# Neighbour attention on one core: the weighted values summed by TensorE instead of VectorE

## The chip, the cores and the metric

The kernel runs on one NeuronCore of a Trainium2 chip. The metric is the device time of one execution in microseconds (us). Three runs of the kernel before took 2073.58, 2077.10 and 2083.18 us; the median is 2077.1 us.

## The reference

There are 3327 nodes with 256 features each and an adjacency matrix that is about 0.24% full, so a node has some eight neighbours besides itself. The reference applies four layers. Layers 0, 2 and 3 are transformer layers over the graph, layer 1 is an average over neighbours that is not touched by the change. A transformer layer is, cut to what matters:

```python
qkv = layer_norm(x, g1, be1) @ w_qkv                 # 8 heads of 32
scores = jnp.einsum('nhd,mhd->hnm', q, k) * SCALE
scores = jnp.where(adj != 0, scores, -jnp.inf)
attn = jax.nn.softmax(scores, axis=-1)
out = jnp.einsum('hnm,mhd->nhd', attn, v).reshape(n, DIM)
x = x + out @ w_proj + b_proj
x = x + jax.nn.gelu(layer_norm(x, g2, be2) @ w1 + b1) @ w2 + b2
```

Everything is float32. Since the matrix is sparse, the kernel does not form the dense scores: it makes a list of neighbours for each node and gathers their keys and values.

## The kernel before

**Stages.** First the adjacency matrix is read, lists of neighbours are made, and the nodes are sorted by their number of neighbours (0 to 306 us in the profile). Then come block 0, the averaging layer, block 1 and block 2. A block is one transformer layer (function `block`). It works on 26 tiles of 128 nodes. Since the nodes are sorted, tile `t` needs at most `ROOM[t]` neighbours: 24 for tile 0, 14 for tile 1, 12 for tiles 2 and 3, down to 4 for tiles 24 and 25, and 228 in sum. The tiles are taken from the smallest to the largest, in ten groups: (25,24), (23,22), (21,20,19), (18 to 15), (14 to 11), (10 to 7), (6,5,4), (3,2), (1), (0).

**Gathering and scoring** (`scores`). A tile loads its own row of keys, values and queries (`own`, three buffers; an indirect load by GpSimd in block 0, a plain load on SyncE's queue in blocks 1 and 2). Its neighbours' keys and values come in units of four neighbours (`unit`, 128 x 4 x 512 float32), each neighbour by one indirect load that GpSimd issues (L546). There are ten unit buffers for the whole block, so the loads run ahead by as many units as are free. ScalarE copies the query into a PSUM bank (L571; two such banks), and the scores lie in the same bank. For each unit VectorE multiplies the keys with the query (L576) and sums over the 32 elements of a head (L577). Then it adds the mask (L591), takes the maximum (L593) and subtracts it (L595); ScalarE takes the exponential (L596).

**Weighing** (`weighed`) is called one tile later, after the scores of the next tile. VectorE sums the exponentials (L605), takes the reciprocal (L606) and scales them (L607). It multiplies the values of `own` and of every unit with them, in place for the units (L610). Then it adds up: full units to the first one (L622), the last, shorter unit as well (L626), the four rows of the first unit in two halvings (L630), and the result to the tile's output `o` (L631). A unit's buffer is free after its last addition.

**The rest of the block** (`project`, `feed_forward`, `end`, `scatter`) goes by groups. TensorE transposes `o` (L658), ScalarE copies the result to SBUF as `oT` (L659), and TensorE multiplies with `w_proj` (L664). VectorE adds it to `x` (L671); after a normalization TensorE transposes (L256) and runs the two feed-forward products (L685, L695), with ScalarE's GELU between them (L688). In block 0 the averaging layer's inputs follow, in block 1 the next layer's keys (L538, L540), and GpSimd scatters the rows (L837, L779, L711). These steps are put off by some tiles through the list `later`, so that they run beside the gathers of later tiles.

**What sets the order.** The framework schedules the instructions on each engine by their order in the program and by its estimate of when they are ready; at run time every engine takes its own queue strictly in that order. An engine that waits holds up all that stands behind it. Float32 products on TensorE appear as two matmul records each in the profile, transposes as one.

The PSUM banks of a block are: four for `mm`, two for `tr` and two for `qs`, which is all eight.

Of the kernel before, what the change touches and what calls it, by code (L numbers as in the profile page):

```python
# [19 lines left out]
BF = mybir.dt.bfloat16  # L20
HF = mybir.dt.float16
F32 = mybir.dt.float32
# [9 lines left out]
P = 128  # L32
CW = 512
N = 3327
DIM = 256
HEADS = 8
HD = DIM // HEADS
# [14 lines left out]
KC = DIM // P  # L52
# [4 lines left out]
SLOTS = 24  # L57
LW = 32
LV = SLOTS + 1
UNIT = 4  # L60
# [25 lines left out]
class Sparse:  # L86
# [5 lines left out]
    def __init__(self, ctx, tc, bad):  # L92
        self.tc, self.nc = tc, tc.nc
        nc = self.nc
        self.bad = bad
        const = ctx.enter_context(tc.tile_pool(name="fixed", bufs=1))
# [23 lines left out]
        self.own = [dram.tile([P, 3 * DIM], F32, tag=f"own{t}", name=f"own{t}") for t in range(NT)]  # L120
        self.ones3 = const.tile([3, P], BF, name="ones3")
        nc.vector.memset(self.ones3, 1.0)
        self.biases = const.tile([3, 6, DIM], BF, name="biases")
        self.to = const.tile([P, NT], U32, name="to")
        self.ranks = dram.tile([NP], F32, name="ranks")
# [426 lines left out]
    def scores(self, pool, pp, layer, t, held):  # L552


        nc = self.nc
# [10 lines left out]
            nc.sync.dma_start(out=own[:, : 3 * DIM], in_=self.own[t])  # L566
        if layer < 2:
            nc.scalar.copy(self.x[t], own[:, 3 * DIM :])
        bank = pp.tile([P, CW], F32, tag="qs", name="qs", bufs=2)
        query = bank[:, :DIM]  # L570
        nc.scalar.copy(query, own[:, 2 * DIM : 3 * DIM])  # L571
        s = bank[:, ds(DIM, (SLOTS + 1) * HEADS)].rearrange("p (j h) -> p j h", h=HEADS)
        units = []

        def dot(at, k, n):
# [20 lines left out]
        nc.scalar.activation(s[:, : J + 1, :], s[:, : J + 1, :], AF.Exp)  # L596
        return own, s, units

    def weighed(self, pool, t, own, s, units):

        nc = self.nc
        J = ROOM[t]
        wide = [P, J + 1, HEADS]
        total = pool.tile([P, HEADS], F32, tag="total", name="total", bufs=3)
        nc.vector.tensor_reduce(total, s[:, : J + 1, :].rearrange("p j h -> p h j"), AX.X, ALU.add)  # L605
        nc.vector.reciprocal(total, total)  # L606
        nc.vector.tensor_mul(s[:, : J + 1, :], s[:, : J + 1, :], total.unsqueeze(1).to_broadcast(wide))  # L607

        def weigh(to, v, at, n):
            nc.vector.tensor_mul(  # L610
                to.rearrange("p j (h d) -> p j h d", d=HD), v.rearrange("p j (h d) -> p j h d", d=HD),
                s[:, ds(at, n), :].unsqueeze(3).to_broadcast([P, n, HEADS, HD]),
            )

        o = pool.tile([P, DIM], F32, tag="o", name="o", bufs=5)
        weigh(o.unsqueeze(1), own[:, DIM : 2 * DIM].unsqueeze(1), 0, 1)
        for u, j0, n in units:
            v = u[:, :n, DIM:]
            weigh(v, v, 1 + j0, n)
        full = [u for u, _, n in units if n == UNIT]  # L620
        for u in full[1:]:
            nc.vector.tensor_add(full[0][:, :, DIM:], full[0][:, :, DIM:], u[:, :, DIM:])  # L622
        u = full[0]
        for r, _, n in units:
            if n < UNIT:
                nc.vector.tensor_add(u[:, :n, DIM:], u[:, :n, DIM:], r[:, :n, DIM:])  # L626
        n = UNIT
        while n > 1:
            n //= 2
            nc.vector.tensor_add(u[:, :n, DIM:], u[:, :n, DIM:], u[:, ds(n, n), DIM:])  # L630
        nc.vector.tensor_add(o, o, u[:, 0, DIM:])  # L631
        return o

    def block(self, layer, weights, then, ahead=None, last=None):

# [3 lines left out]
        with tc.tile_pool(name="bs", bufs=1) as pool, tc.tile_pool(name="bp", bufs=1, space=PSUM) as pp:  # L639
            begin, finish, write = then(pool, pp) if then else (None, None, None)  # L640
            held = self.held

            def attended(t, own, s, units):
                o = self.weighed(pool, t, own, s, units)
                return t, o

            def halves(name, n):

                banks = [pp.tile([P, CW], F32, tag="mm", name=name, bufs=4) for _ in range(0, n, 2)]
                return [banks[q // 2][:, ds(q % 2 * DIM, DIM)] for q in range(n)]  # L650

            def project(group, outs):
                w = len(group) * P
                ps = [pp.tile([P, CW], F32, tag="tr", name="otr", bufs=2) for _ in range(KC)]
                oT = pool.tile([P, KC, CW], F32, tag="hT", name="oT", bufs=2)
                for k in range(KC):
                    for q, (t, o) in enumerate(outs):
                        nc.tensor.transpose(ps[k][:, ts(q, P)], o[:, ts(k, P)], self.ident)  # L658
                    nc.scalar.copy(oT[:, k, :w], ps[k][:, :w])  # L659
                ys = halves("proj", len(group))  # L660
                for q, y in enumerate(ys):
                    self.bias(y, 2 * layer)
                    for k in range(KC):
                        nc.tensor.matmul(y, oT[:, k, ts(q, P)], wpj[:, k, :], start=False, stop=k == KC - 1)  # L664
                return ys
# [67 lines left out]
                        scatter(group, ys)  # L733
                    later.sort(key=lambda x: (x[0], -x[1]))

            waiting, step, outs = None, 0, []
            for group in [*GROUPS, ()]:
                for t in group or (None,):
                    now = t is not None and (group, t, *self.scores(pool, pp, layer, t, held))
                    if waiting:  # L740
                        done, *rest = waiting
                        outs.append(attended(*rest))
                        if len(outs) == len(done):
                            later.append((step + 1 + (len(done) > 2), 0, done, project(done, outs)))
                            later.sort(key=lambda x: (x[0], -x[1]))
                            outs = []
                    waiting = now
                    if begin and step == 2:
                        begin()
                    run(step)  # L750
                    step += 1
# [829 lines left out]
```

## Time and profile before

| What | Value |
| --- | --- |
| Median of three runs | 2077.1 us |
| Profiled execution, first to last instruction | 2094.6 us |
| Mean granted TensorE clock | 0.770 of full speed |
| VectorE busy | 1342.0 us (64%) |
| TensorE busy, matmuls | 1263.4 us (60%) |
| GpSimd busy | 1001.0 us (48%) |
| ScalarE busy | 684.9 us (33%) |
| Indirect loads of neighbours (L546), 684 | 667.2 us, 975 ns each |
| Dot products (L576, units and own), 276 | 244.0 us |
| Weighing (L610, units and own), 276 | 242.2 us |

The profile is one execution, taken by the hardware's profiler. PE is TensorE's matmuls, PEld its weight loads, DVE VectorE, ACT ScalarE, POOL GpSimd and SP SyncE. A line such as L546 is a line of the kernel before. In a row of a group, `out<-in` names the tiles, then come the shapes and the count; after the bar stand the busy time and the mean time of one in ns, after the next bar the idle time of that engine just before these instructions, with the work that ended it. The three blocks' 228 loads each lie at 314 to 760, 1071 to 1484 and 1609 to 2002 us; the rest of a block, until its last feed-forward is through, lasts until about 850, 1606 and 2095 us.

### The profile page before, as it was taken

To read this page: it belongs to the slowest core of one execution; us is meant where nothing else is said; L and a number is where in the kernel's file an instruction comes from. 1 tells how busy PE (TensorE), PEld (TensorE's weight loads), DVE (VectorE), ACT (ScalarE), POOL (GpSimd) and SP (SyncE) were. 2 spreads that over 40 slices of the span, in tenths; PEclk is the share of its full clock that TensorE was granted. 3 is DMA by queue.
4 is the path that set the end of the run, shared out by engine and by line. 5 is a ranking of instruction groups with operands and counts; after the bars stand their busy time and mean duration, and the time that the engine had idled before them with its cause. 6 is when DMAs were issued, how large, how long until landed. Compare 5 with 4: busy or idle time off the path is not lost. (4 is left out here: it accounts for less than half of the span.)

```text
span 2094.6 us, 17222 instructions
## 1 busy us (share of the span) xinstructions
PE 1263.4 (60%) x4806; PEld 812.1 (39%) x4806; DVE 1342.0 (64%) x3407; ACT 684.9 (33%) x1420; POOL 1001.0 (48%) x946
## 2 busy tenths in 40 slices
PE   3244411556755579699934688567695277655676
PEld 1122200344424337577512454343473154323445
DVE  3567635577776785165636789776732679976871
ACT  3555501233321224122322444334343133322232
POOL 3768757555555531101156645555203666565521
PEclk8667655677767769799976888798798587767778
DMA  8878827555555550858486656656215665565520
GB/s 191 330 300 326 284 79 213 160 163 154 170 148 175 147 131 23 198 154 230 160 284 205 216 166 209 220 178 193 61 56 201 210 186 176 176 190 160 152 65 20
DMA packets 169409, 369.73 MB, mean 177 GB/s; under 512 B 78821, under 2 KB 90291, under 8 KB 165976
## 3 DMA queue, kind: packets, MB, share of 16 engines
q0 software_dynamic: 68624, 222.01, 35.4%
q1 hardware_dynamic: 85689, 112.44, 17.1%
q10 hardware_dynamic: 14990, 34.08, 5.0%
q8 instruction: 40, 0.66, 0.1%
q14 instruction: 66, 0.54, 0.1%
HBM read 279.77 MB, written 77.59 MB: 171 GB/s over the span
## 5 line engine op out<-in xcount | busy, mean ns | idle before, releaser
L546 POOL DMA_INDIRECT unit<-kv,ids x684 | 667.2, 975 | 434.7 <-issue 189.1
L685 PE MATMUL f<-hT,w 128*128 128x256 f32 (+3 forms) x960 | 342.1, 517 | 58.6 <-ACT gT L688 23.2
L256 PE MATMUL tr<-ident,xh 128*128 128x128 f32 x312 | 80.6, 384 | 442.7 <-ACT xh L251 395.6
L695 PE MATMUL f<-w,gT 128*128 128x256 f32 x1248 | 306.4, 399 | 17.9 <-ACT gT L688 14.3
L685 PEld LDWEIGHTS f<-hT,w 128*128 128x128 f32 x960 | 190.4, 219 | 202.6 <-issue 106.0
L695 PEld LDWEIGHTS f<-w,gT 128*128 128x128 f32 x1248 | 238.3, 197 | 68.7 <-ACT gT L688 18.3
L256 PEld LDWEIGHTS tr<-ident,xh 128*128 128x128 f32 x312 | 41.7, 179 | 483.3 <-ACT xh L251 414.8
L576 DVE TENSOR_TENSOR unit<-unit,qs 128x1024 f32<-128x1024 f32 (+3 forms) x198 | 211.7, 1069 | 26.4 <-DMA unit<-kv,ids 15.0
L577 DVE TENSOR_REDUCE qs<-unit 128x32 f32<-128x1024 f32 (+3 forms) x198 | 212.7, 1074 | 4.8 <-DVE qs L607 1.7
L610 DVE TENSOR_TENSOR unit<-unit,qs 128x1024 f32<-128x1024 f32 (+3 forms) x198 | 210.0, 1065 | 0.0
L315 POOL TENSOR_TENSOR m<-a,place 128x3328 f16<-128x3328 fp8e4 x26 | 159.4, 6132 | 78.7 <-ACT a L313 78.6
L688 ACT ACTIVATE gT<-f,b 128x256 f32<-128x256 f32 (+3 forms) x240 | 124.8, 536 | 212.5 <-PE f L685 106.6
L538 PE MATMUL kvps<-wqkv,hT 128*128 128x512 f32 x312 | 171.9, 677 | 29.5 <-ACT hT L262 22.5
L326 DVE MAX8 found<-m 128x8 f16<-128x416 f16 x208 | 111.5, 579 | 39.7 <-POOL m L315 33.1
L664 PE MATMUL proj<-wproj,oT 128*128 128x256 f32 x312 | 109.3, 489 | 42.7 <-ACT oT L659 22.8
L576 DVE TENSOR_TENSOR own<-own,qs 128x256 f32<-128x256 f32 x78 | 32.3, 415 | 141.5 <-ACT qs L571 124.2
L658 PE MATMUL otr<-ident,o 128*128 128x128 f32 x156 | 25.5, 289 | 142.4 <-DVE qs L577 87.4
L990 POOL DMA_INDIRECT sorted<-st,to x26 | 24.8, 955 | 178.7 <-ACT st L542 147.1
L538 PEld LDWEIGHTS kvps<-wqkv,hT 128*128 128x128 f32 x312 | 63.2, 213 | 86.7 <-issue 37.7
L313 ACT ACTIVATE a<-a 128x3328 fp8e4<-128x3328 int32 x26 | 77.3, 2973 | 51.6 <-DMA kv<-st 29.0
L251 ACT ACTIVATE xh<-x,shift,rstd 128x256 f32<-128x256 f32 x104 | 58.4, 594 | 104.5 <-DVE shift L218 80.9
L664 PEld LDWEIGHTS proj<-wproj,oT 128*128 128x128 f32 x312 | 66.9, 235 | 65.6 <-ACT oT L659 28.4
(193 smaller groups left out, 1881.4 us busy)
## 6 DMA issues: line engine op xcount, KB each, us to landing
a<-in_adj SPq DMA_DIRECT2D x25, 1663.5 KB
kv<-st ACTq DMA_DIRECT2D x52, 512.0 KB
own<-sorted SPq DMA_DIRECT2D x26, 512.0 KB
unit<-kv,ids POOLq DMA_INDIRECT x684
adj<-a SPq DMA_DIRECT2D x26, 416.0 KB
own<-qkv SPq DMA_DIRECT2D x26, 384.0 KB
own<-own SPq DMA_DIRECT2D x26, 384.0 KB
w<-in_L_gnn_w SPq DMA_DIRECT2D x6, 1024.0 KB
```

The source lines that it names most:

```text
L256: nc.tensor.transpose(ps[k][:, ts(q, P)], t[:, ts(k, P)], self.ident)
L315: nc.gpsimd.tensor_mul(m.rearrange("p (s e) -> p s e", e=SEG), a8.rearrange("p (s e) -> p s e", e=SEG), place.unsqueeze(1).to_broadcast([P ...
L326: nc.vector.max(found[:, i, s, :], m[:, ts(s, SEG)])
L538: nc.tensor.matmul(kv, hT[:, k, ts(q, P)], w[:, k, DIM : 3 * DIM], start=k == 0, stop=k == KC - 1)
L546: g = self.nc.gpsimd.indirect_dma_start(out=out, out_offset=None, in_=table, in_offset=bass.IndirectOffsetOnAxis(ap=self.ids[:, t, j : j + ...
L576: nc.vector.tensor_mul(k, k, query.unsqueeze(1).to_broadcast([P, n, DIM]))
L577: nc.vector.tensor_reduce(s[:, ds(at, n), :].rearrange("p j h -> p (j h)"), k.rearrange("p j (h d) -> p j h d", d=HD), AX.X, ALU.add,)
L610: nc.vector.tensor_mul(to.rearrange("p j (h d) -> p j h d", d=HD), v.rearrange("p j (h d) -> p j h d", d=HD), s[:, ds(at, n), :].unsqueeze ...
L664: nc.tensor.matmul(y, oT[:, k, ts(q, P)], wpj[:, k, :], start=False, stop=k == KC - 1)
L685: nc.tensor.matmul(y[:, :w], w1[:, k, ts(f, P)], hT[:, k, :w], start=k == 0, stop=k == KC - 1)
L688: nc.scalar.activation(gT[-1][:, f % 2, :w], y[:, :w], AF.Gelu_apprx_tanh, bias=b1[:, f : f + 1])
L695: nc.tensor.matmul(y, gT[f // 2][:, f % 2, ts(q, P)], w2[:, f, :], start=False, stop=f == FC - 1)
```

## The change

The query is no longer copied: the dot products read it from `own` in SBUF. The scores lie in an SBUF tile with three buffers. The two PSUM banks of `qs` go to a tile `acc`. VectorE still multiplies the values with the weights, now in place for `own` too, but it no longer adds them up. Instead TensorE multiplies every weighted row of 128 nodes x 128 features with the identity and accumulates in `acc`, two products per neighbour (one for each half of the features), after one small product of ones and zeros that clears the tile. As the weighted rows are the stationary operand, `acc` comes out transposed, so the transposes (L658) go, and ScalarE copies `acc` of each tile into its part of `oT`. The lines below are numbered anew in the changed kernel.

```diff
+        self.zeros3 = const.tile([3, DIM], BF, name="zeros3")
+        nc.vector.memset(self.zeros3, 0.0)
...
-        bank = pp.tile([P, CW], F32, tag="qs", name="qs", bufs=2)
-        query = bank[:, :DIM]
-        nc.scalar.copy(query, own[:, 2 * DIM : 3 * DIM])
-        s = bank[:, ds(DIM, (SLOTS + 1) * HEADS)].rearrange("p (j h) -> p j h", h=HEADS)
+        query = own[:, 2 * DIM : 3 * DIM]
+        s = pool.tile([P, SLOTS + 1, HEADS], F32, tag="s", name="s", bufs=3)
...
+        acc = pp.tile([P, KC, P], F32, tag="acc", name="acc", bufs=2)
+        nc.tensor.matmul(acc.rearrange("p k r -> p (k r)"), self.ones3, self.zeros3, start=True, stop=False)
+
+        def weigh(v, at, n):
             nc.vector.tensor_mul(
-                to.rearrange("p j (h d) -> p j h d", d=HD), v.rearrange("p j (h d) -> p j h d", d=HD),
+                v.rearrange("p j (h d) -> p j h d", d=HD), v.rearrange("p j (h d) -> p j h d", d=HD),
                 s[:, ds(at, n), :].unsqueeze(3).to_broadcast([P, n, HEADS, HD]),
             )
-
-        o = pool.tile([P, DIM], F32, tag="o", name="o", bufs=5)
-        weigh(o.unsqueeze(1), own[:, DIM : 2 * DIM].unsqueeze(1), 0, 1)
+            for j in range(n):
+                for k in range(KC):
+                    nc.tensor.matmul(
+                        acc[:, k, :], v[:, j, ts(k, P)], self.ident, start=False, stop=at + j == J and k == KC - 1
+                    )
+
+        weigh(own[:, DIM : 2 * DIM].unsqueeze(1), 0, 1)
         for u, j0, n in units:
-            v = u[:, :n, DIM:]
-            weigh(v, v, 1 + j0, n)
-        full = [u for u, _, n in units if n == UNIT]
-        for u in full[1:]:
-            nc.vector.tensor_add(full[0][:, :, DIM:], full[0][:, :, DIM:], u[:, :, DIM:])
-        u = full[0]
-        for r, _, n in units:
-            if n < UNIT:
-                nc.vector.tensor_add(u[:, :n, DIM:], u[:, :n, DIM:], r[:, :n, DIM:])
-        n = UNIT
-        while n > 1:
-            n //= 2
-            nc.vector.tensor_add(u[:, :n, DIM:], u[:, :n, DIM:], u[:, ds(n, n), DIM:])
-        nc.vector.tensor_add(o, o, u[:, 0, DIM:])
-        return o
+            weigh(u[:, :n, DIM:], 1 + j0, n)
+        return acc
...
+            def attended(group, q, t, own, s, units):
+                acc = self.weighed(pool, pp, t, own, s, units)
+                if q == 0:
+                    turned[group] = pool.tile([P, KC, CW], F32, tag="hT", name="oT", bufs=2)
+                nc.scalar.copy(turned[group][:, :, ts(q, P)], acc)
...
-                ps = [pp.tile([P, CW], F32, tag="tr", name="otr", bufs=2) for _ in range(KC)]
-                oT = pool.tile([P, KC, CW], F32, tag="hT", name="oT", bufs=2)
-                for k in range(KC):
-                    for q, (t, o) in enumerate(outs):
-                        nc.tensor.transpose(ps[k][:, ts(q, P)], o[:, ts(k, P)], self.ident)
-                    nc.scalar.copy(oT[:, k, :w], ps[k][:, :w])
+                oT = turned.pop(group)
```

## The prediction

> **What bounds the kernel now.** I read the page's busy times first, then busy time by stretch, then the groups of the three blocks, then the waits.
>
> ```profile
> span 2094.6 us, 17222 instructions
> ...
> PE 1263.4 (60%) x4806; PEld 812.1 (39%) x4806; DVE 1342.0 (64%) x3407; ACT 684.9 (33%) x1420; POOL 1001.0 (48%) x946
> ```
>
> No engine fills the span, so the limit has to be found by stage. Each block has a gather phase (its 228 indirect loads) and a tail after the last of them; from the trace they lie at 314-760 and 760-850, 1071-1484 and 1484-1606, 1609-2002 and 2002-2095. Busy time in those stretches (columns: length, then busy time and count by engine, granted clock, DMA):
>
> ```profile
> core 0: us, PE busy (x) PEld busy (x) DVE busy (x) ACT busy (x) POOL busy (x), PEclk, DMA share, GB/s
> 314.00:584.00 270.00, 137.37 (x490) 92.24 (x491) 188.56 (x440) 77.41 (x179) 159.83 (x165) 0.71 0.59 173
> 584.00:760.00 176.00, 98.49 (x321) 61.24 (x321) 124.68 (x248) 43.19 (x106) 99.26 (x102) 0.70 0.54 155
> 760.00:850.00 90.00, 75.38 (x341) 54.42 (x341) 48.70 (x136) 35.23 (x98) 10.73 (x12) 0.86 0.29 77
> 1071.00:1340.00 269.00, 162.26 (x524) 100.69 (x525) 202.37 (x487) 98.97 (x227) 154.55 (x157) 0.75 0.65 205
> 1340.00:1484.00 144.00, 104.35 (x339) 61.54 (x337) 102.48 (x195) 51.06 (x100) 84.59 (x86) 0.88 0.61 192
> 1484.00:1606.00 122.00, 101.07 (x395) 67.46 (x395) 51.67 (x153) 57.53 (x145) 10.96 (x12) 0.89 0.25 82
> 1609.00:1825.00 216.00, 112.81 (x367) 72.87 (x368) 167.78 (x382) 62.03 (x131) 133.35 (x135) 0.69 0.63 194
> 1825.00:2002.00 177.00, 105.70 (x349) 65.34 (x347) 129.69 (x253) 40.60 (x83) 106.66 (x108) 0.75 0.57 167
> 2002.00:2095.00 93.00, 64.30 (x282) 45.90 (x280) 46.67 (x110) 29.60 (x71) 11.04 (x11) 0.85 0.09 26
> ```
>
> In the gather phases VectorE is busy 313 of 446, 305 of 413 and 297 of 393 us (70 to 76%). GpSimd is busy 259, 239 and 240; with the 0.3 us that it loses before every issue it is at 332, 307 and 307 (74 to 78%). TensorE has 236, 267 and 218 (53 to 65%). In the tails TensorE leads (69 to 84%). So a loop of VectorE, GpSimd and the ten unit buffers paces the gather phases, and the last feed-forwards on TensorE pace the tails.
>
> **The additions that go.** L622, L626, L630 and L631:
>
> ```profile
> L622 DVE TENSOR_TENSOR unit<-unit 128x1024 f32<-128x1024 f32 x66 | 80.2, 1216 | 0.0
> ...
> L630 DVE TENSOR_TENSOR unit<-unit 128x512 f32<-128x512 f32 (+1 forms) x156 | 86.1, 552 | 4.4 <-DVE qs L591 1.2 <-issue 1.1 <-DVE qs L577 1.0
> ```
>
> With L626 (37.0 us) and L631 (32.5) that is 235.8 us, 79 a block, of which 66 lie in the gather phase. VectorE's gather phases fall to 247, 239 and 231 us.
>
> **The query copies that go.** L571 costs ScalarE 29.2 us, and VectorE waits for it:
>
> ```profile
> DVE own L576 <- ACT qs L571: 124.2, 22, 24.4
> ...
> ACT qs L571 <- DVE unit L610: 78.2, 17, 14.1
> ```
>
> The copy waits for one of two PSUM banks, which the weighing (L610) of two tiles earlier gives back. The new dot reads `own` and an SBUF tile with three buffers, so this wait goes. What is late next is `own` itself in block 0 (ScalarE waits 86.5 us for it at L568 already), and elsewhere the gathers. The part that comes back is at most 124 us and at least nothing; it is inside the phase estimate below, not added to it. The per-tile copies of `acc` (78, by L571's 0.375 us some 29 us) replace 60 copies of 23.8 us, beside other work on ScalarE. But each is a new wait in ScalarE's queue: behind it stand the GELUs and the next exponential, and VectorE's L605 waits for that.
>
> **The products that come.** Per block 228+26 rows of values, two halves each: 508 products of 128x128 f32 and 26 zeroing products. Each f32 matmul of this kernel is two records (L695: 26 tiles x 8 x 3 blocks = 624 in the code, x1248 in the trace), while a transpose is one (L658: 52 x 3 = 156). The nearest row, the same shape at the full clock:
>
> ```profile
> 2064.14 3.84 PE L685 MATMUL f<-hT,w 128*128 128x128 f32 x32 [0.50 <-ACT hT L262]
> ```
>
> 3.84/32 = 0.12 us a record, 0.24 a product, 122 us a block; with 26 zeroings by the bias product's 0.12 us spacing (+3) and 52 transposes gone (25.5/3 = -8.5), +117 us. At half clock wider records of this line take twice as long (128x384: 2.93 us for four at 763.7, 4.14 for twelve at 781.7), so the other end is +230. I take +117, since a busier TensorE should hold its clock (0.85 to 0.89 in the tails, 0.70 to 0.75 where it is half idle). The Trainium skill ("TensorE: Matmul & The Clock Gate", Terms) calls transpose mode four times faster for fp32; an estimate by it, four records' time a product, makes 244 us a block. The trace's two records decide against it.
>
> Of the 122 us, tiles 1 and 0 (80 products, 19 us) fall into the tail, since in the new order they stand behind the feed-forward of (6,5,4) and of (3,2). The gather phases get 95: TensorE goes to 331 of 446, 362 of 413, 313 of 393 us, if nothing stretched. In block 1, which also makes keys, that is 88%. And TensorE moves into the buffer loop: a unit is free not after VectorE's addition but after its products, which stand in order behind a feed-forward. One for four tiles holds TensorE from 1959.6 to 1986.2, 27 us. `own` too is now given back by a product: the loads of the next `own`, on SyncE's queue in blocks 1 and 2 and on GpSimd's in block 0, wait for TensorE with it. The other way round, a product that waits for VectorE's weighing holds up the feed-forward queued behind it, and VectorE's L671 and GpSimd's scatters wait for that. These waits have no row of their own; the phase shares below carry them.
>
> **Both operands in SBUF.** Gathers take 0.946 us, unless VectorE is at an addition with both inputs in SBUF:
>
> ```profile
> 743.83 1.88 POOL L546 DMA_INDIRECT unit<-kv,ids  x1 [3.36 <-DVE qs L595]
> ```
> ```profile
> 743.67 1.22 DVE L622 TENSOR_TENSOR unit<-unit 128x1024 f32<-128x1024 f32 x1
> ```
>
> The gather that began 0.16 us into the addition took 1.88 us: it ends about 0.82 us after the addition. Over the trace a gather that starts inside such an instruction is lengthened by what remains of it less 0.125 us; none is lengthened by L576, L577 or L610, which have one operand in PSUM. After the change L576 and L610 (487 us) have both inputs in SBUF and the additions (236 us) are gone. Putting that rule on the old positions of all 788 indirect DMAs gives 26 us for the additions (the rows show 684 x 0.029 = 20 for the unit gathers) and 92 us for L576, L610 and the small score steps: +66 us, 22 a block, to GpSimd: 354, 329, 329 with its issue gaps. Bounds: -20 if the gathers fall into step with VectorE and nothing is left, and 684 x 0.41 (162 us of such instructions in a 400 us phase) x 0.49 us (mean remainder of 1.21 us less 0.125) = 137, so 117 more than now, if they start anywhere. I take the count on the real positions. The Trainium skill ("SBUF — State Buffer", Who interferes with whom) says the later of the two blocks for the whole instruction, and speaks against this change; by it the same count without the 0.125 us would be somewhat higher. VectorE itself loses nothing visible: 1.22 us at most under a gather.
>
> **The sum.** In the gather phases the busiest engine after the change is GpSimd (354), TensorE (362), GpSimd (329, TensorE 313). Now the best is 78% (GpSimd in block 2). At 78% the phases would be 454, 464 and 422 us: +8, +51, +29 = +88. At 88% they would be 402, 411 and 374: -44, -2, -19 = -65. Three engines near 80% in strict order will not reach the second; a rising clock shortens TensorE's older work and helps. I take 82.5%: 429, 439, 399, in sum +15. The tails are TensorE's: +19 us each, less the 7.5 us of additions after tile 0's weighing where TensorE waited for them; bounds 0 and 19, taken 12: +35. ScalarE's and SyncE's own queues: nothing added on the path. The two stages outside the blocks are untouched.
>
> Sum +50 us on the profiled execution's 2094.6 us span (the page shows no time around it): 2145. That execution is 17.5 us above the median of the runs, 2077.1, so the forecast is 2077.1 + 50 = 2127 us. A measurement of this kernel tells some 0.5% (10 us) from no change.
>
> **Rivals.**
> - *VectorE's relief comes through.* For it: VectorE is the busiest engine in the gather phases, loses a fifth there, and its 124 us wait for queries goes. Against: it leaves GpSimd at 329 to 354 and puts TensorE beside it. It decides from 86%: there the phases are 412, 421, 383 (-37), which the tails' +35 just cancel. At 90%, 393, 402, 366 (-91) and +35: 2021 us.
> - *The unit buffers wait behind TensorE.* Tiles of 9 to 12 gathers take three of the ten buffers, so little more than three tiles are in flight. At 22 us a tile (584-760 for the last eight or so) a 27 us feed-forward ahead of the products holds the buffers of one to two tiles; if GpSimd then stops for 12 us at four such places a block, that is 144 us, of which I count a third as inside the idle time that 82.5% leaves anyway: +96 over the sum's +50, 2223 us. It decides from about three stops a block. For it: GpSimd's waits for L622 and L631, which release units, are 119 us already. Against: tiles of up to 8 gathers take two buffers and have slack.
> - *Even.* Gain in blocks 0 and 2, loss in block 1 and the tails: 2077.
> - That the change does not do what it says is excluded by the program's own order: no addition is left on VectorE, and the products stand in TensorE's queue.
>
> **How the numbers follow.** Forecast 0.52 (2090 to 2185), relief 0.27 (1960 to 2066), unit buffers 0.13 (2185 to 2320), even 0.08. The range leaves out the lower part of the relief and the upper part of the buffers' case, about a tenth each: 2000 to 2205. Faster is the relief, 0.27; same is the even case, 0.08; slower the other two, 0.65.
>
> **What would show it.** No additions on VectorE, 288, 278 and 265 us of it left in the three blocks (367, 357, 344 now); 3048 new records on TensorE, near 0.12 us apart; gathers longer than 1 us in far more than 76 cases; TensorE above 75% in the gather phases with a clock above 0.8; GpSimd waiting for TensorE at the gathers instead of VectorE; tails longer by 10 to 20 us. Wrong if products run at half clock throughout (then slower), if the gathers keep 0.946 us, or if the gather phases fall below 400 us each (then VectorE was the limit).

## The result, and the profile after

The changed kernel took 2229.3 us (median of four runs, 2211.0 to 2236.4), the kernel before 2076.5 us on the same chip: 1.073 times as long, with a 95% interval of 1.066 to 1.079. The forecast of 2127 us had the sign right and was 102 us short; its range ended at 2205.

The profiled execution of the changed kernel, from its page:

```profile
span 2234.7 us, 22841 instructions
...
PE 1588.0 (71%) x7776; PEld 1170.7 (52%) x7776; DVE 1162.3 (52%) x3054; ACT 681.0 (30%) x1372; POOL 1081.4 (48%) x946
```

VectorE lost 180 us, TensorE won 325, and the span grew by 140. Busy time by stretch, each block from its first to its last gather and then its tail (columns as in the prediction):

```profile
core 0: us, PE busy (x) PEld busy (x) DVE busy (x) ACT busy (x) POOL busy (x), PEclk, DMA share, GB/s
313.00:792.00 479.00, 339.37 (x1658) 258.07 (x1659) 270.47 (x598) 126.82 (x274) 290.49 (x266) 0.82 0.52 155
792.00:880.00 88.00, 80.33 (x482) 67.73 (x480) 31.73 (x106) 31.41 (x90) 10.84 (x13) 0.97 0.31 78
1107.00:1588.00 481.00, 367.21 (x1720) 268.00 (x1721) 268.45 (x605) 152.50 (x334) 260.28 (x243) 0.85 0.55 173
1588.00:1699.00 111.00, 102.82 (x527) 78.16 (x525) 29.25 (x112) 48.49 (x118) 10.67 (x12) 1.00 0.27 92
1699.00:2134.00 435.00, 313.18 (x1556) 241.58 (x1556) 259.46 (x559) 105.19 (x206) 267.85 (x243) 0.83 0.55 164
2134.00:2235.00 101.00, 77.25 (x427) 63.14 (x427) 23.00 (x68) 27.53 (x62) 10.99 (x12) 0.87 0.09 24
```

The gather phases took 446, 413 and 392 us and take 479, 481 and 435: 143 us more, which is the whole loss. No engine is busy for more than 77% of any of them. GpSimd, which issues the gathers, is busy for 819 us in the three phases and was for 738: 80 of the 143 us are longer work on it, and 63 are longer waiting. Its 684 gathers, before and after, with their busy time, mean time and the idle time ahead of them:

```profile
L546 POOL DMA_INDIRECT unit<-kv,ids x684 | 667.2, 975 | 434.7 <-issue 189.1
```
```profile
L548 POOL DMA_INDIRECT unit<-kv,ids x684 | 739.8, 1082 | 468.0 <-issue 192.5
```

The waits of GpSimd, VectorE and ScalarE in the changed kernel (what waits, for what: us in total, times, longest):

```profile
POOL unit L548 <- PE acc L619: 186.4, 25, 27.7
...
POOL out L703 <- DVE x L663: 124.7, 10, 38.2
...
DVE unit L576 <- DMA unit<-kv,ids: 189.4, 64, 21.3
DVE x L663 <- PE f L687: 153.7, 30, 12.1
...
ACT oT L641 <- PE acc L619: 276.9, 36, 19.4
```

GpSimd waits 186 us for products (L619) before it may load into a unit again; before, it waited 119 us for the additions that freed units:

```profile
POOL unit L546 <- DVE o L631: 64.4, 11, 8.2
POOL unit L546 <- DVE unit L622: 54.7, 10, 14.3
```

With what is put down to other work, its waits of over 0.4 us at a unit's gather sum to 229 us in the three phases before and to 256 after. The rest of its new waiting is mostly in block 2, where scatters of finished rows (L703) stand in GpSimd's queue ahead of gathers and need the feed-forward's result. In that block's gather phase they cost more than the products, and 7.0 us before the change:

```profile
POOL out L703 <- DVE x L663: 49.9, 6, 16.0
POOL unit L548 <- PE acc L619: 35.2, 9, 27.7
```

VectorE waits 189 us for gathered units (15 before) and 154 us for feed-forward results (73 before). One wait for products, on TensorE's timeline (start, duration, then the work; `x` is the number of records):

```profile
523.52 1.51 PE L619 MATMUL acc<-ident,unit 128*128 128x128 f32 x8
524.88 7.03 PE L677 MATMUL f<-hT,w 128*128 128x512 f32 x16
534.56 8.83 PE L677 MATMUL f<-hT,w 128*128 128x512 f32 x16 [2.65 <-ACT gT L680]
...
543.53 3.72 PE L687 MATMUL f<-w,gT 128*128 128x256 f32 x16
...
555.12 3.72 PE L687 MATMUL f<-w,gT 128*128 128x256 f32 x16
558.67 2.17 PE L619 MATMUL acc<-ident,unit 128*128 128x128 f32 x18
```

The products stop at 525 us for a feed-forward of four tiles and go on at 558.67. By then VectorE had weighed six more units:

```profile
525.71 2.69 DVE L613 TENSOR_TENSOR unit<-unit,s 128x1024 f32<-128x1024 f32 x3
...
540.36 2.69 DVE L613 TENSOR_TENSOR unit<-unit,s 128x1024 f32<-128x1024 f32 x3
```

On GpSimd and on ScalarE in the same stretch:

```profile
559.33 0.95 POOL L548 DMA_INDIRECT unit<-kv,ids  x1 [24.78 <-PE acc L619]
```
```profile
560.88 0.37 ACT L641 COPY oT<-acc 128x256 f32<-128x256 f32 x1 [16.76 <-PE acc L619]
```

GpSimd had no free unit for 24.8 us and issued its next gather 0.7 us after the products went on. Over all 198 units, the lag, which is the time from a unit's weighing to the end of its last product, is 28.8, 31.9 and 28.2 us in the mean of the three blocks, and 57 at most. That matmuls keep their program order is also what the Trainium skill states ("PSUM — Partial Sum Buffer", Engine vs sequencer instructions); the row of 558.67 is what it costs here.

### The profile page after: what moved, and what is told of

Its sections match the earlier page's. It is cut to its first block, busy times and chain, and to the rows that moved or that the text cites. A ratio compares the mean times of both kernels' runs of the same rounds, so it can differ in the third digit from the quotient of the medians.

```text
span 2234.7 us, 22841 instructions
## 1 busy us (share of the span) xinstructions
PE 1588.0 (71%) x7776; PEld 1170.7 (52%) x7776; DVE 1162.3 (52%) x3054; ACT 681.0 (30%) x1372; POOL 1081.4 (48%) x946
## 4 chain that ended last, share of the span: by engine, by line
PE 45%; issue 12%; DMA 11%; DVE 11%; another core or an unknown queue 9%; ACT 6%; POOL 5%; SPq 0%; ACTq 0%; DVEq 0%; POOLq 0%
PE f L687 10%; PE f L677 10%; PE acc L619 9%; PE kvps L540 5%; POOL unit L548 4%; DMA kv<-st 4%; PE qps L542 2%; DVE unit L576 2%; DMA unit<-kv,ids 2%; DVE s L577 2%; PE proj L656 2%; PE tr L258 2%; DMA st<-in_x 2%; PE tf L966 1%
## 5 line engine op out<-in xcount | busy, mean ns | idle before, releaser
L548 POOL DMA_INDIRECT unit<-kv,ids x684 | 739.8, 1082 | 468.0 <-issue 192.5
L619 PE MATMUL acc<-ident,unit 128*128 128x128 f32 x2736 | 370.9, 292 | 45.3 <-issue 42.3
L619 PEld LDWEIGHTS acc<-ident,unit 128*128 128x128 f32 x2736 | 355.9, 208 | 54.6 <-issue 51.7
L576 DVE TENSOR_TENSOR unit<-unit,own 128x1024 f32<-128x1024 f32 (+3 forms) x198 | 212.6, 1077 | 236.2 <-DMA unit<-kv,ids 189.4
L677 PE MATMUL f<-hT,w 128*128 128x256 f32 (+3 forms) x960 | 301.9, 473 | 23.8 <-issue 11.2
L577 DVE TENSOR_REDUCE s<-unit 128x32 f32<-128x1024 f32 (+3 forms) x198 | 209.5, 1065 | 0.3
L613 DVE TENSOR_TENSOR unit<-unit,s 128x1024 f32<-128x1024 f32 (+3 forms) x198 | 205.0, 1073 | 0.0
L619 PE MATMUL acc<-ident,own 128*128 128x128 f32 x312 | 65.6, 338 | 131.2 <-DVE own L613 98.7
L619 PEld LDWEIGHTS acc<-ident,own 128*128 128x128 f32 x312 | 51.7, 229 | 169.1 <-issue 89.3
L576 DVE TENSOR_TENSOR own<-own 128x256 f32<-128x256 f32 x78 | 33.1, 424 | 158.5 <-DMA own<-kv,ids 48.2
```

What stands on the lines that cost most here:

```text
L548: g = self.nc.gpsimd.indirect_dma_start(out=out, out_offset=None, in_=table, in_offset=bass.IndirectOffsetOnAxis(ap=self.ids[:, t, j : j + ...
L576: nc.vector.tensor_mul(k, k, query.unsqueeze(1).to_broadcast([P, n, DIM]))
L577: nc.vector.tensor_reduce(s[:, ds(at, n), :].rearrange("p j h -> p (j h)"), k.rearrange("p j (h d) -> p j h d", d=HD), AX.X, ALU.add,)
L613: nc.vector.tensor_mul(v.rearrange("p j (h d) -> p j h d", d=HD), v.rearrange("p j (h d) -> p j h d", d=HD), s[:, ds(at, n), :].unsqueeze( ...
L619: nc.tensor.matmul(acc[:, k, :], v[:, j, ts(k, P)], self.ident, start=False, stop=at + j == J and k == KC - 1)
L677: nc.tensor.matmul(y[:, :w], w1[:, k, ts(f, P)], hT[:, k, :w], start=k == 0, stop=k == KC - 1)
```

## The experiments

Theory A says that this holding of units behind TensorE is the loss. Theory B puts it on the longer gathers (both operands of VectorE's products in SBUF), Theory C on the sum of TensorE's work, Theory D on ScalarE's copies of the sums, which wait in its queue ahead of later tiles' exponentials.

Kernels of one set ran on one chip, beside the kernel before. Chips differ: the kernel before took 1910 to 1914 us on the chips of four sets, 2088 on that of the third set, and 2076 where the result was measured. So ratios to the kernel before on the same chip are compared, and ratios of different sets only where these chips were alike. "Excess" is the time of the 684 unit gathers over 946 ns each.

### First set: one part alone, and less of the sums

The move to SBUF alone (`b_sbuf`):

```diff
-        bank = pp.tile([P, CW], F32, tag="qs", name="qs", bufs=2)
-        query = bank[:, :DIM]
-        nc.scalar.copy(query, own[:, 2 * DIM : 3 * DIM])
-        s = bank[:, ds(DIM, (SLOTS + 1) * HEADS)]...
+        query = own[:, 2 * DIM : 3 * DIM]
+        s = pool.tile([P, SLOTS + 1, HEADS], F32, tag="s", name="s", bufs=3)
```

> The kernel before with one part of the change alone: the queries are read where they land in SBUF and the scores are a tile in SBUF; ScalarE's 78 query copies go, VectorE's additions stay, TensorE gets no products. Theory A (units wait behind TensorE: the products stand in TensorE's order behind the feed-forward, so the ten unit buffers come free some 30 us later): this part brings only the longer gathers, some 60 to 75 us of GpSimd time over the three blocks, of which a part is hidden: 2077 to 2150 us, best guess 2110, and well below the 2229 us of the changed kernel. Theory B (VectorE's products with both operands in SBUF hold up GpSimd, and this alone is the loss): 2200 to 2230 us. Theory C (TensorE has too much work in the gather phases) as A.

Measured 1.038 (1.033 to 1.042), 72 us. The group of the gathers in that kernel, from its page:

```profile
L546 POOL DMA_INDIRECT unit<-kv,ids x684 | 820.1, 1199 | 224.0 <-issue 169.8
```

1199 ns a gather: 173 us of excess, of which 66 belong to gathers that began under the dot products, 66 under the weighing and 36 under the additions. GpSimd never waits long for a unit here; it is busy or issuing for 398 of the first gather phase's 411 us. So this part costs 72 us by itself, by making GpSimd the limit. That is less than half of what the changed kernel loses on a like chip (1.083, next set), so Theory B alone fails; but it is also a little above A's range (2150 for 2077, 1.035).

TensorE sums only one unit a tile (`a_hyb`):

```diff
+        total_of(weigh(own[:, DIM : 2 * DIM].unsqueeze(1), 0, 1), 1, False)
+        for u, j0, n in units:
+            weigh(u[:, :n, DIM:], 1 + j0, n)
+        first = units[0][0]
+        for u, _, n in units[1:]:
+            nc.vector.tensor_add(first[:, :n, DIM:], first[:, :n, DIM:], u[:, :n, DIM:])
+        total_of(first[:, :, DIM:], UNIT, True)
```

> The changed kernel, but VectorE adds all units of a tile into its first one, and TensorE sums only the own row and the four rows of that unit: 26 x 10 = 260 products a block in place of 508. All units but the first come free by VectorE's work, as before the change; the copy of the turned sum stays. Theory A: the first unit of each tile still waits (26 of 83 units a block), the others do not: 2100 to 2160 us. Theory B (longer gathers): not below 2229, rather 2240, since the additions are work more for VectorE. Theory C: some 57 us less TensorE work a block, 2130 to 2180.

Measured 1.0185 (1.013 to 1.024), with 135 us of excess. VectorE has 120 additions (117 us) more than in the changed kernel, and yet the time is far shorter, as A and C said and B did not. It is inside A's range (1.011 to 1.040) and below C's (1.026 to 1.050).

Half of the products, so that half of the features are left out of each sum (`a_half`):

```diff
-                for k in range(KC):
-                    nc.tensor.matmul(acc[:, k, :], v[:, j, ts(k, P)], self.ident, ...)
+                nc.tensor.matmul(acc[:, j % KC, :], v[:, j, ts(j % KC, P)], self.ident, ...)
```

> The changed kernel with one of the two products of each row (the sum over half of the features is left out, so the attention's output is partly zero): 254 products a block where there were 508, some 58 us less of TensorE's work a block; the feed-forward in front of them is untouched. Theory A: the lag falls only by the products' own part, from 30 to some 24 us, and the time by 20 to 60 us, to 2170 to 2210. Theory B (longer gathers): no change, 2215 to 2245. Theory C (sum of TensorE's work decides): the whole of it, some 100 to 150 us, to 2080 to 2130.

Measured 1.058 (1.053 to 1.063), inside A's range (1.045 to 1.064) and above C's (1.001 to 1.026). The lag fell to 21.0, 18.5 and 16.6 us.

### Second set: the same work in another order

The kernel before and the changed kernel again (`before_2`, `after_2`), without an edit:

> The kernel before, unchanged, profiled on the chip of these runs, since chips differ: in the first runs it took 1913 us where it had taken 2077. All theories: within 0.5% of the kernel before. What is looked for is the mean of its 684 gathers and how long GpSimd waits for VectorE's additions: Theory B (longer gathers are most of the loss) needs gathers near 975 ns here too.

> The changed kernel, unchanged, on the chip of these runs. All theories: 1.06 to 1.08 times the kernel before if the ratio does not depend on the chip; GpSimd's idle time before gathers put down to the products 150 to 200 us, gathers near 1080 ns.

Measured 1907 us, gathers at 982 ns; and 1.083 (1.078 to 1.089), gathers at 1104 ns (108 us of excess), 129.5 us of GpSimd's time before gathers put down to products. The loss is a little larger on this chip, the wait somewhat smaller than expected.

The feed-forward in pieces (`a_split2`):

```diff
                 for f in range(FC):
+                    if f == FC // 2 and cut(group):
+                        yield None
...
+                if cut(group):
+                    yield None
                 ys = halves("f2", len(group))
                 for q, y in enumerate(ys):
+                    if q == 2 and cut(group):
+                        yield None
```

Each `yield` puts the rest off by one tile.

> The changed kernel with the feed-forward of the groups from tiles 21 to 7 (15 of 26 tiles, 116 of 228 gathers a block) cut into four pieces (half of the first product's slices, the other half, the second product for two tiles, for the others), each issued one tile later than the one before: TensorE does the same work, but there the products of a tile stand behind some 9 us of feed-forward at a time, where it was up to 34 us. Theory A (units wait behind TensorE): the lag from a unit's weighing to the end of its last product falls from 30 us to 15 to 20, GpSimd's wait for products by half or more, and the ratio to the kernel before from 1.073 to 1.03 to 1.05. Theory B (longer gathers) and Theory C (the sum of TensorE's work): no change, 1.065 to 1.08.

Measured 1.060 (1.054 to 1.065): 43 us less with the same work on every engine. GpSimd's wait for products fell from 129.5 to 87.9 us. That speaks for the order and against B and C. But A's numbers missed: less than half of the loss came back, and the mean lag did not fall (26.2, 31.1 and 24.4 us against 24.9, 26.0 and 21.2). By groups it did fall for tiles 18 to 15 (24.2 to 16.8 us) and 14 to 11 (29.0 to 17.1). It stayed for the other two divided groups (27.7 to 28.1 and 24.7 to 27.1) and rose for the last two tiles (17.0 to 62.1 and 30.4 to 47.4), which hold 10 of a block's 66 units. In the profiled executions the gather phases became 89 us shorter, and all that lies outside them 44 us longer: half of the gain was lost there again.

Weighed values in tiles of their own (`a_f16x2u8`; the identity is halved, since each product is issued twice):

```diff
-UNITS = 10
+UNITS = 8
...
-        def weigh(v, at, n):
+        def weigh(values, at, n):
+            v = pool.tile([P, UNIT, DIM], HF, tag="wv", name="wv", bufs=8)[:, :n, :]
...
-                for k in range(KC):
+                for k, h in ((k, h) for k in range(KC) for h in range(2)):
```

> The changed kernel with the weighed values written to float16 tiles of their own (8 of them, in the place of two of the ten unit buffers) and summed from there, each product twice with half the identity in float16: a unit is free when VectorE has weighed it, as TensorE's lag falls on the small tiles; VectorE reads and TensorE's records are as many as in the changed kernel. Theory A (units wait behind TensorE): a unit's life falls from 66 us to some 35, GpSimd's waits for products are gone, and the ratio to the kernel before falls from 1.073 to at most 1.045, near the 1.038 of the kernel with the move to SBUF alone. Theory B (longer gathers): 1.065 to 1.08. Theory C (the sum of TensorE's work): 1.07 if a record keeps its 114 ns, and not below 1.055, the ratio with half of the products, if it takes half of that.

Measured 1.043 (1.038 to 1.049). The products and the gathers of that kernel, from its page:

```profile
L551 POOL DMA_INDIRECT unit<-kv,ids x684 | 758.5, 1109 | 296.5 <-issue 178.7
...
L623 PE MATMUL acc<-identh,wv 128*128 128x128 f16 x3048 | 231.8, 239 | 153.8 <-DVE wv L617 69.2
```

The excess is that of the changed kernel (111 us), so B has nothing to do with the 77 us that came back. Records now follow at 56 ns, not 112, so TensorE's work fell as well, about as far as with half of the products: its busy time in the gather phases is 292, 310 and 266 us here and 304, 312 and 273 there. With the units still held (`a_half`, on another chip that is alike) that was worth 1.083 to 1.058; the release of the units, though there are two fewer, brings the rest, to 1.043, which is below the 1.055 that Theory C allowed.

### Third set: queries and scores back in PSUM

Four kernels on the slower chip. The control frees two PSUM banks (`a_mm3a1`), the next puts queries and scores there (`a_qs3a1`):

```diff
-        acc = pp.tile([P, KC, P], F32, tag="acc", name="acc", bufs=2)
+        acc = pp.tile([P, KC, P], F32, tag="acc", name="acc", bufs=1)
...
-                banks = [pp.tile([P, CW], F32, tag="mm", name=name, bufs=4) ...
+                banks = [pp.tile([P, CW], F32, tag="mm", name=name, bufs=3) ...
```

> The control of the next run: the changed kernel with three matmul banks in place of four and one bank for the sums in place of two, so that two PSUM banks are free and unused. All theories: no faster than the changed kernel, 1.08 to 1.11 times the kernel before on a chip where the changed kernel takes 1.083, since ScalarE's copy of a sum now also holds up the next tile's products. Theory D (ScalarE's copies of the sums hold TensorE up) the upper end or more.

> The same as the control, but queries and scores lie in two PSUM banks again, and ScalarE copies the queries there, as before the change: TensorE's products and sums stay as in the changed kernel. Theory B (longer gathers): the gathers' mean falls from 1100 ns to at most 990, 80 us less of GpSimd's time, and the ratio by 0.03 to 0.045 below the control. Theory A (units wait behind TensorE): gathers fall as much, but GpSimd waits longer for units in exchange, and the ratio falls by at most 0.015.

Measured 1.075 (1.067 to 1.084) for the control, a little less than expected, and 1.114 (1.106 to 1.121) with the queries and scores in PSUM: 3.8% of the kernel before slower, where both theories expected a gain. The gathers did what was foreseen (page of `a_qs3a1`), and VectorE's waits in the same kernel show the price:

```profile
L548 POOL DMA_INDIRECT unit<-kv,ids x684 | 649.4, 949 | 568.5 <-PE acc L621 291.6
```
```profile
DVE own L578 <- ACT qs L573: 145.9, 27, 25.3
DVE total L608 <- ACT qs L598: 135.8, 31, 17.6
```

At 949 ns there is no excess left, 85 us of GpSimd's time are saved, and it waits 292 us for products. ScalarE must again copy each query (L573) before VectorE may begin a tile, and in ScalarE's queue that copy and the exponential (L598) stand behind copies of sums, which wait for products. VectorE waits 282 us for the two; in the control it has no query copies to wait for, and waits 31 us for exponentials. So the query copy and sums on TensorE do not go together in this order of the queues, and reading the query from SBUF is what keeps the changed kernel from being slower still.

Both cures (`a_f16qs`: the third set's banks, and float16 weighed values with one product each) and the divided sum with queries in PSUM (`a_hybqs`: the edits of `a_hyb` and `a_qs3a1`):

> Both cures at once: queries and scores in PSUM (three matmul banks, one bank for the sums), weighed values in eight float16 tiles with eight units, each product once in float16. VectorE has no additions, the gathers are short, units come free at the weighing and the products take a quarter of the time (56 ns records, one each). Theories A and B together: what each adds goes, 1.043 less some 0.03: 0.99 to 1.02 times the kernel before. Theory C (the sum of TensorE's work): 0.98 to 1.01. If the scores' banks or the eight units bind instead: 1.02 to 1.05.

> VectorE adds a tile's units into its first one, TensorE sums that unit's four rows and the own row (260 products a block), queries and scores in PSUM with ScalarE's query copies (three matmul banks, one for the sums). Against the run of the same division of the sum with queries and scores in SBUF (1.0185) the gathers are short again: Theory B (longer gathers, mean 1143 ns there, now near 975) gives 0.97 to 0.995, Theory A 0.99 to 1.02, since most units came free by VectorE there already.

Measured 1.069 (1.062 to 1.076) and 1.022 (1.013 to 1.030). The first misses by far and the second lies just above A's range, though gathers take 947 and 969 ns and most units come free by VectorE. It fits that each tile still passes through ScalarE behind copies of sums: in the first, VectorE waits 125 us for exponentials and 74 for query copies. No run takes this wait away by itself.

### Fourth set: how many units each kernel needs

Eight units (`a_u8`, `b_u8`):

```diff
-UNITS = 10
+UNITS = 8
```

> The changed kernel with eight unit buffers in place of ten. Theory A (units wait behind TensorE): a unit is held some 60 us and a block has 66 of them, so a phase cannot be shorter than 60 x 66 / 8 = 495 us if the holding stays as it is: 1.10 to 1.16 times the kernel before, and at least twice the loss that the kernel before has with eight units; far above the 1.043 of the kernel that had eight units but released them at the weighing. Theory D (ScalarE's copies of the sums hold up the tiles behind them): units are not what binds, and both kernels lose alike, at most 0.03.

> The kernel before with eight unit buffers in place of ten, the control of the run above. Theory A: its units are held less long, so it loses 0.01 to 0.04. Theory D: as much as the changed kernel loses.

Measured 1.164 (1.159 to 1.170) for the changed kernel and 0.999 (0.997 to 1.002) for the kernel before, where a loss of 0.01 to 0.04 was expected. The group of the gathers in the changed kernel with eight units, with what ended the idle time, and then in the kernel before with eight:

```profile
L548 POOL DMA_INDIRECT unit<-kv,ids x684 | 749.7, 1096 | 539.3 <-PE acc L619 227.7 <-issue 177.2 <-DVE x L663 88.4
```
```profile
L546 POOL DMA_INDIRECT unit<-kv,ids x684 | 668.0, 977 | 343.3 <-issue 162.8 <-DVE unit L622 59.7 <-DVE qs L595 20.3
```

This shows what the units are worth. The kernel before has two to spare: without them its units are held less long (41.5, 38.6 and 35.0 us from the first gather to the weighing, against 51.7, 45.3 and 39.8 in `before_2`). In the changed kernel a unit is held for 53.9, 55.1 and 50.2 us with eight and 58.2, 58.4 and 51.6 with ten (`after_2`), from gather to last product, so fewer units mean fewer gathers. At eight, block 1 needs 55.1 x 66 / 8 = 455 of its 490 us for its 66 units. And eight units freed at the weighing (1.043) lose much less than eight held by products (1.164).

The copy of a sum one tile later (`a_late`; the projection and the feed-forward follow it):

```diff
                     now = t is not None and (group, t, *self.scores(...))
+                    if summed:
+                        copied(*summed)
...
                     if waiting:
                         done, *rest = waiting
-                        attended(done, outs, *rest)
+                        summed = attended(done, outs, *rest)
```

> The changed kernel with ScalarE's copy of a tile's sum (and what follows it, the projection of the group and its feed-forward) issued one tile later, behind the next tile's exponential and ahead of the next sum's products: nothing else moves. Theory D (the copies): ScalarE's waits for sums fall from some 500 us to under 200, and the ratio from 1.075 to 1.03 to 1.05. Theory A (units wait behind TensorE): the products stay where they were, at most 0.015 less.

Measured 1.114 (1.109 to 1.119), slower by 3 points than the changed kernel on a like chip, where Theory D expected a gain: moving the copies is no cure. ScalarE's waits in this kernel:

```profile
ACT less L212 <- DVE x L665: 299.9, 34, 18.5
ACT s L596 <- DVE s L595: 171.1, 35, 19.5
ACT oT L643 <- PE acc L619: 171.0, 36, 18.6
```

The wait for sums went from 265 to 171 us, and the wait for VectorE's `x` (L212) from 156 to 300: the later projection moved the wait along, so this run does not tell what the copies alone cost.

All of it together (`a_lfs`: the edits of `a_late`, `a_split2`, and float16 tiles with eight units and one product each):

> Queries and scores in SBUF as in the changed kernel, but with the copies one tile later, the weighed values in eight float16 tiles with eight units (each product once, in float16), and the feed-forward cut into four pieces: all waits on TensorE and ScalarE relieved together. Theories A and D together: what is left is the longer gathers, so near the kernel with the move to SBUF alone (1.038) less what VectorE's additions are worth: 1.00 to 1.035. If the longer gathers or the eight units bind: 1.035 to 1.05.

Measured 1.046 (1.041 to 1.051), not the gain that was expected. GpSimd hardly stops in its gather phases of 390, 372 and 349 us, with 114 us of excess; outside them it takes 879 us, where `before_2` takes 830.

### Fifth set: what is left

The same without the late copies (`a_fs`), that with the scores in PSUM and the query in SBUF (`a_fsp`, with the third set's three matmul banks and one bank for the sums), and the kernel before with the same placing (`b_s`). The tile of the scores in `a_fsp`; `b_s` has the same new line:

```diff
-        s = pool.tile([P, SLOTS + 1, HEADS], F32, tag="s", name="s", bufs=3)
+        s = pp.tile([P, SLOTS + 1, HEADS], F32, tag="s", name="s", bufs=2)
```

> As the run with late copies, float16 weighed values in tiles of their own, eight units and divided feed-forward (1.046), without the late copies. If its remaining loss lay between the gather phases, where that run was some 50 us longer than the kernel before: 1.015 to 1.03. Theory B (longer gathers are the rest): no change in the gather phases, whose sum was 36 us above the kernel before; 1.02 to 1.045.

> The run beside it with the scores in two PSUM banks, three matmul banks in place of four and one for the sums in place of two; the queries stay in SBUF, so that ScalarE has no query copies. The weighing then has one operand in PSUM, and the gathers' excess over 946 ns should fall from some 113 us to 60. Theory B: 50 us less of GpSimd's time, 0.015 to 0.025 below the run beside it. If something else binds (the one bank for sums, TensorE): no change or slower.

> The kernel before with queries in SBUF (no query copies) and scores in PSUM: VectorE's additions stay, TensorE gets no products. Of the gathers' excess of 173 us with both in SBUF (1.038), the dot products' 77 us stay and the weighing's 67 us go. Theory B: about half of the loss, 1.00 to 1.025. If the loss of that run was not the gathers: 1.03 to 1.04 again.

Measured 1.0295 (1.024 to 1.036), 1.0035 (1.001 to 1.006) and 0.998 (0.995 to 1.002). The gathers of the first and of the second, from their pages' groups with what ended the idle time:

```profile
L550 POOL DMA_INDIRECT unit<-kv,ids x684 | 753.9, 1102 | 257.8 <-issue 175.7 <-DVE wv L616 44.9 <-DMA unit<-kv,ids 14.3
```
```profile
L550 POOL DMA_INDIRECT unit<-kv,ids x684 | 704.9, 1031 | 271.5 <-issue 172.5 <-DVE wv L616 58.4 <-DMA unit<-kv,ids 18.6
```

Taking the scores out of SBUF saved 49 us of gathers and 47 us of time. The two need not be the same microseconds: the profiled executions differ by 38 us, of which 22 lie in the gather phases and 16 outside. But where units come free at the weighing, GpSimd is near its limit: in `a_fs` it is busy or issuing for 375, 335 and 347 us of gather phases of 390, 358 and 356. In the kernel before an excess of 98 us is free (`b_s`), while 173 us cost 72: up to about a hundred is covered there, with the query copies gone. No version beat the kernel before.

The loss on a like chip, 1.083, thus goes in steps that were measured on two like chips, each of which changes more than one thing: release of the units and the shorter products -0.040, divided feed-forward and single products -0.014, scores in PSUM -0.026, and 0.0035 is left.

## Why the prediction was right or wrong

- **The sum's third term, the phases at 82.5%, failed.** The step reads "these waits have no row of their own; the phase shares below carry them", and then "I take 82.5%: 429, 439, 399, in sum +15". Measured: 479, 481 and 435, +143, with the busiest engine at 76, 76 and 78% (GpSimd with its issue gaps, 366 and 337 us, in blocks 0 and 2, TensorE in block 1). That is about the low end that I had worked out, 78%, and there the sum was +88 already. A share taken from the kernel before does not carry a new wait in the loop of the buffers, which held each unit 28 to 32 us beyond its weighing while no engine came near full. Nor could it hold two losses at once: the gathers under two operands in SBUF cost 0.038 by themselves, and with two units fewer the changed kernel loses another 0.081 and the kernel before nothing.
- **The rival was the case.** "The unit buffers wait behind TensorE" gave 2223 us; 2229 was measured. It had 0.13, far too little. It counted four stops of 12 us a block; the trace has 16 over 0.42 us in three blocks, 184 us in all, 11.5 each. That its total came so near is partly luck: it had +111 us for the gather phases and +35 for the tails, where +143 and -5 were measured, and the scatters' waits in block 2 were named in the prediction but priced nowhere. Its feed-forward of 27 us, read from a view that began at 1960, starts at 1954.62 and holds TensorE for 31.6. What I set against it, that small tiles have slack, is refuted by the pair with eight units: the changed kernel has none, though the kernel before has.
- **The rule for two operands in SBUF held in its size, not in its weight.** The count gave 92 us of excess over all 788 indirect loads; 92.7 was measured for the 684 of the units alone, and 155 of these exceed 1000 ns (76 before). So close a match is partly luck, since the rule counted what remains of one instruction, and the gathers at other times meet whole runs of them (last section). And this was put beside other work within a share, while alone it costs 72 us. The Trainium skill ("SBUF — State Buffer", Who interferes with whom) lets instructions with at most one SBUF input pass without a conflict, and the excess under the weighing did go when the scores moved to PSUM.
- **The additions that go** were summed as 236 us from the groups' durations; VectorE's busy time fell by 180, since records of instructions in sequence overlap: without the additions' records, the trace before has VectorE busy for 1159 of its 1342 us. In the gather phases it is at 270, 268 and 259 us, where 247, 239 and 231 were forecast.
- **The products** were right in kind: 3048 records, most of them 112 ns apart (2447 intervals) and some 213 (358 of 190 to 245), TensorE at 339, 367 and 313 us against the forecast 331, 362 and 313, clock 0.82 to 0.85. That these match is partly luck: products and clearings keep TensorE busy for 444 us, 148 a block where 125 were forecast, while its other work without the transposes went from 1244 to 1175 us. "TensorE above 75%" held in block 1 alone, as the phases grew.
- **The tails, +35, failed.** They are 5 us shorter in sum (88, 111 and 101 us after 90, 122 and 93). TensorE does have the late products there, but the last gathers come so late that more of the other work is done by then; that is argued from the order of the work, and no run tests it.
- **The query copies**: their removal was called part of the estimate, at least nothing. The third set shows more: with sums on TensorE, keeping them, with the scores in PSUM, costs 3.8%, even though it frees the gathers.

## What to carry to other kernels

Before moving work to an engine with room, ask which buffer that work will hold and what stands ahead of it in that engine's queue; price the buffer's whole round trip, not the engines' shares. Taking away a few buffers in the kernel before and after is a cheap test of whether that trip is the limit. And if the moved work must read a scarce buffer, copy its input out on the engine that last touches it, so that the buffer comes free there; here that, with shorter products, took the ratio from 1.083 to 1.043.

## What the runs showed of the hardware

A gather is held up not by one VectorE instruction with both operands in SBUF but by a whole run of them. On GpSimd and on VectorE in the changed kernel:

```profile
516.44 4.48 POOL L548 DMA_INDIRECT unit<-kv,ids  x1 [0.30 <-issue]
```
```profile
516.28 2.35 DVE L613 TENSOR_TENSOR unit<-unit,s 128x1024 f32<-128x1024 f32 x2
518.55 0.41 DVE L576 TENSOR_TENSOR own<-own 128x256 f32<-128x256 f32 x1
518.89 1.21 DVE L576 TENSOR_TENSOR unit<-unit,own 128x1024 f32<-128x1024 f32 x1
520.02 0.41 DVE L577 TENSOR_REDUCE s<-own 128x8 f32<-128x256 f32 x1
```

The gather began inside the first of four such instructions and ended 0.82 us after the last, at 520.92. The three other longest gathers end 0.82 us after their runs too. The sums over one input (L577) let it pass. The same kernels took 9% longer on some chips than on others, while VectorE's busy time in the gather phases was nearly the same (313, 305 and 297 us in the kernel before on the slower chip, 315, 307 and 303 in `before_2`); the runs don't tell why.
